# Attention kernel on one core: the end of the last group, with a's last products behind b's and the second half's b part added on GpSimd

## The chip, the cores and the metric

The kernel runs on one core of a Trainium2 chip. The time is that of one execution on the device, in microseconds (us); before the change it is 2299.06 us, the median of 3 runs (2298.87 to 2299.11). The engines are TensorE (PE; its weight loads are PEld), VectorE (DVE), ScalarE (ACT), GpSimd (POOL) and SyncE (SP, which issues most DMAs). An engine's name with a q (SPq, PEldq) is its sequencer, which handles waits, loads of registers and branches.

## The reference

```
q = x Wq + bq;  k = x Wk + bk;  v = x Wv + bv          # x is 4 x 64 x 64 x 256, N = 4096
pq, pk, pv = q, k, v, each reshaped to (B, -1, N)
attention = softmax(pq^T pk) over the keys m
out = pv attention^T, reshaped to x's shape
return gamma * out + x                                   # gamma is one number
```

For each of the 4 images, x and the result count as a matrix of 256 rows and 4096 columns. Everything is float32.

## The kernel before, in words

**Splitting.** TensorE multiplies in a rounded float32 format (F32R). Each operand is therefore split in a high part h, a low part l and a part d that holds a combination of both, and a float32 product is made of three products. For the attention they are gathered in two sums: `a` (products of h and of l) and `b` (products of d). The result is gam2 * a + gam1 * b, where gam1 and gam2 carry gamma and the factors of the split (lines 651 and 652).

**Units.** The queries of an image are cut in 8 groups of 512 columns, the keys in 16 blocks of 256. A *unit* n is one group with one block; there are 4 x 8 x 16 = 512 units, 0 to 511, and the loop at line 701 goes over them. For a unit, `cross` and `energy` make the energies on TensorE and exponentiate them on ScalarE (x); `upper` makes h on ScalarE; `halves` adds x to the group's sum s on VectorE (line 415), and makes l and d there (lines 430 and 432). After a group's last unit, `whole` adds the two halves of s (line 421). `attend(n, j, order)` multiplies with v: j = 0 and 1 are the two halves of the result's rows, and `order` says which of h, l, d (0, 1, 2) are multiplied, in which order. With h and l it adds to `now["a", j]`, with d to `now["b", j]`; both lie in PSUM and gather over the 16 units of a group. Each part is two matmuls of 128x512.

**Order.** The program is written in the order in which each engine executes it (manual schedule): every engine works through its own list, and waits on semaphores where a tile comes from another engine. In a turn of the loop, TensorE does attend(n, 0) and later attend(n, 1); `halves(n + 1)` stands between them.

**The end.** For all groups but the last, the sums are taken out of PSUM by `emptied` and finished by `finish` in pieces, by DMAs and VectorE, beside the next group's work. The last group has no next one; at unit 511 the loop calls `finish_last(n, xr)` (line 521) and stops. There:
- four matmuls of s with ones (zp, lines 525 to 529) give the sums of the exponentials with the queries on the partitions; line 532 takes the reciprocals into rall;
- attend(511, 0) is multiplied; ScalarE scales a of the first half into y0 (line 535);
- `inside` (lines 518 and 519) and line 538 test whether all reciprocals of all groups are in range, into zs;
- four matmuls with the identity (rp, line 541) spread the reciprocals over all partitions, in PSUM; one (np, line 549) adds up zs;
- attend(511, 1) is multiplied, its b part first; ScalarE scales b of the second half into y1 (line 551);
- VectorE adds b to y0 (552), sets the flag `again` from np (553), multiplies y0 by rp (554), adds it to x's first half in xr (555), and SyncE stores that half (556);
- the same for the second half (557 to 560).

x's last group was loaded into xr at unit 506 (line 712). Behind all this every engine reads `again` and branches (line 764): if a reciprocal was out of range, a second, plain version of the whole computation runs; with these inputs it is jumped over. 

**Tiles that matter here.** zp and rp share two PSUM buffers with the energies (tag "e"); np has one of its own. `o_last` is one buffer in SBUF, with y0 and y1. The tiles of tag "x" are two buffers in SBUF of 128 x 2 x 512, used by turns; the last exponentials lay in them.

Of the kernel before, what the change touches and what calls it, by code (L numbers as in the profile page):

```python
# [9 lines left out]
F32 = mybir.dt.float32  # L10
F32R = mybir.dt.float32r
I32 = mybir.dt.int32
AF = mybir.ActivationFunctionType
ALU = mybir.AluOpType
AX = mybir.AxisListType
# [5 lines left out]
def kernel(  # L21
# [36 lines left out]
    nc = tc.nc  # L58
    B, W, H, C = x.shape
    P = 128  # L60
# [21 lines left out]
    NB = 512  # L82
    NJ = NB // P
    NG = N // NB
    NU = NM // 2
    STEPS = NG * NU
# [5 lines left out]
    ones = ones_r.bitcast(F32)  # L92
    again = const.tile([P, 1], I32, name="again")
    gam3 = const.tile([P, 3], F32, name="gam")
    gam, gam1, gam2 = (gam3[:, i : i + 1] for i in range(3))
    zs = const.tile([P, 1], F32, name="zs")
    rall = const.tile([P, B * NG, NJ], F32, name="rall")
# [3 lines left out]
    with ExitStack() as fast:  # L101
# [5 lines left out]
        ppool = pool("ppool", 2)  # L107
        work = pool("work", 2)
        kpool = pool("kpool", 3)
        dram = pool("dram", 2, space=DRAM)  # L110
        ps_e = pool("ps_e", 2, space=PSUM)
# [35 lines left out]
        qd, kf, vf, units, loads, now = {}, {}, {}, {}, {}, {}  # L147
# [259 lines left out]
        def halves(n):  # L407
            if n >= B * STEPS:
                return
            x, h = units[n]  # L410

            def summed():
                if n % NU:
                    s = now["s"]
                    nc.vector.tensor_tensor(s, s, x, ALU.add)  # L415
                else:
                    now["s"] = x

            def whole():
                s = now["sum"] = now["s"]  # L420
                nc.vector.tensor_tensor(s[:, 0, :], s[:, 0, :], s[:, 1, :], ALU.add)

            after = 0 < n < 5
            if not after:
                summed()
            if n % NU == NU - 1:
                whole()
            ld = ppool.tile([P, 2, 2, NB], F32R, tag="ld", name=f"ld_{n}")
            l, d = ld[:, 0], ld[:, 1]
            nc.vector.tensor_tensor(l, x, h.bitcast(F32), ALU.subtract)  # L430

            nc.vector.scalar_tensor_tensor(  # L432
                d, h.bitcast(F32), 1.0 + E, x, ALU.mult, ALU.subtract
            )
            if n == 2:
                next(vs)
                next(vs, None)
            if after:
                summed()
            units[n] = h, l, d  # L440

        def attend(n, j, order=(0, 1, 2)):

            t = n % NU
            if t == 0:
                for i, c in enumerate("ab"):
                    pool, tag = ps_o, f"{c}{j}"
                    if j and n >= (B - 1) * STEPS and n // NU % 2 == 0:
                        pool, tag = now["banks"][i]
                    now[c, j] = pool.tile([P, NB], F32, tag=tag, name=f"{c}{j}_{n // NU}")  # L450
            for f in order:
                to = now["ab"[f == 2], j]
                for i in (1, 0) if f == 1 else (0, 1):
                    nc.tensor.matmul(  # L454
                        to,
                        vall[:, t, i, f, j * P : (j + 1) * P],
                        units[n][f][:, i, :],
                        start=(t == 0 and i == 0 and f != 1),
                        stop=(t == NU - 1 and f != 0 and i == f // 2),
                        skip_group_check=True,  # L460
                    )
# [54 lines left out]
        def inside(ok, r):  # L516

            nc.vector.tensor_scalar(ok, r, 1.0 / Z_HIGH, None, ALU.is_ge)
            nc.vector.scalar_tensor_tensor(ok, r, 1.0 / Z_LOW, ok, ALU.is_le, ALU.mult)

        def finish_last(n, xr):

            b, g = B - 1, NG - 1
            S = now["sum"][:, 0, :]
            zp = ps_e.tile([P, NJ, 2], F32, tag="e", name="zp")
            for j in range(NJ):
                nc.tensor.matmul(  # L527
                    zp[:, j, :], S[:, j * P : (j + 1) * P], ones[:, :2], start=True, stop=True
                )
            attend(n, 0)  # L530
            r4 = rall[:, B * NG - 1, :]
            nc.vector.reciprocal(r4, zp[:, :, 0])
            o = work.tile([P, 2, NB], F32, tag="o", name="o_last", bufs=1)
            y0, y1 = o[:, 0, :], o[:, 1, :]
            nc.scalar.activation(y0, now["a", 0], AF.Identity, scale=gam2)  # L535
            ok = ppool.tile([P, 2, NB], F32, tag="x", name="last")[:, 0, : B * NG * NJ]
            inside(ok, rall.rearrange("p n j -> p (n j)"))
            nc.vector.tensor_reduce(zs, ok, AX.X, ALU.min)
            rp = ps_e.tile([P, NB], F32, tag="e", name="rp")
            for j in range(NJ):  # L540
                nc.tensor.matmul(
                    rp[:, j * P : (j + 1) * P],
                    r4[:, j : j + 1].to_broadcast([P, P]),
                    ident,
                    start=True,
                    stop=True,
                )
            np_ = ps_p.tile([P, 1], F32, tag="p0", name="np")
            nc.tensor.matmul(np_, ones, zs, start=True, stop=True)
            attend(n, 1, (2, 0, 1))  # L550
            nc.scalar.activation(y1, now["b", 1], AF.Identity, scale=gam1)
            nc.vector.scalar_tensor_tensor(y0, now["b", 0], gam1, y0, ALU.mult, ALU.add)  # L552
            nc.vector.tensor_scalar(again, np_, P - 0.5, None, ALU.is_lt)
            nc.vector.tensor_tensor(y0, y0, rp, ALU.mult)
            nc.vector.tensor_tensor(xr[:, 0, :], xr[:, 0, :], y0, ALU.add)
            nc.sync.dma_start(og[b, g][:, 0], xr[:, 0, :])
            nc.vector.scalar_tensor_tensor(y1, now["a", 1], gam2, y1, ALU.mult, ALU.add)  # L557
            nc.vector.tensor_tensor(y1, y1, rp, ALU.mult)  # L558
            nc.vector.tensor_tensor(xr[:, 1, :], xr[:, 1, :], y1, ALU.add)
            nc.sync.dma_start(og[b, g][:, 1], xr[:, 1, :])  # L560


        R = 2 * STEPS // NI
# [137 lines left out]
        for n in range(B * STEPS):  # L701
            b, u = divmod(n, STEPS)
            g, t = divmod(u, NU)
            final = n == B * STEPS - 1
            if n == 0:
                image(1)
                load_x(1, 0)
            if u == STEPS - 5 and b + 2 < B:
                image(b + 2)
            if n == B * STEPS - 6:  # L710
                xr = ppool.tile([P, 2, NB], F32, tag="s", name="xr")
                nc.sync.dma_start(xr, xg[b, g])
            cross(n + LOOK)
            turn = t == NU - 1 and not final
            if t == 0 and n:
                upper(n + LOOK - 1)
            p = n - 3 + 2 * (n > 17)
            step(p, "act")
            late = n >= (B - 1) * STEPS
            if not final:  # L720
                attend(n, 0)
            if late and 1 <= t <= 2 and n > 1:
                emptied(n - 1 - t, 1, done, t - 1)
            energy(n + LOOK)
            load_k(n + LOOK + 3)
            store()
            if t == 0 and n:
                done = full
            if turn:
                emptied(n, 0)  # L730
            else:
                upper(n + LOOK)
            step(p, "pe")
            if turn:
                active.append(finish(n // NU, now["o"], now["s"]))
            if t == 0 and n and not late:
                emptied(n - 1, 1, done, vector=True)
            halves(n + 1)
            step(p, "dve")
            if final:  # L740
                finish_last(n, xr)
                break
            attend(n, 1)
            full = now["a", 1], now["b", 1]
            if n == 17:
                for engine in ("act", "pe", "dve"):
                    step(p + 1, engine)
                    step(p + 2, engine)
            if t == 8 and n + NU < B * STEPS:
                load_q(*divmod(n // NU + 1, NG))  # L750
            for m in range(2 * NU):
                c, r = divmod(n + NU - 3 - 13 * m // 16, STEPS)
                if r == 0 and 0 < c < B:
                    load_v(c, m // 2, m % 2)
            proceed()
            for to, pieces in xloads[:6]:
                nc.sync.dma_start(to, pieces)
            del xloads[:6]

    NB = 512  # L760
    NG = N // NB
    NJ = NB // P
# [213 lines left out]
```

## Time and profile before

| | |
|---|---|
| median of 3 runs | 2299.06 us |
| profiled execution: time | 2299.0 us |
| profiled execution: span, first to last instruction | 2297.2 us |
| mean granted clock of TensorE | 0.999 |
| TensorE's share of the chain that ended last | 99% |
| last matmul pair of 128x512 starts | 2287.69 us |
| last store issued by SyncE | 2290.66 us |

The profile is one execution, taken by the hardware. Its lines give busy time in us for each engine and its share of the span; x10568 is a number of instructions. In the timeline a row is: start in us from the span's beginning, duration in us, engine, line of the kernel, operation, tile written <- tiles read, shapes, and how many instructions the row merges. A [0.46 <-DVE v L160] at its end says that the engine sat idle for 0.46 us before it, until that work of VectorE released it. The chain of work that ended last is followed back from the last instruction, at each step to what released it, or to the instruction before it on its engine. The rows of a single line (L764, the flag) give min/median/max of the duration in ns, and the first and the last start in us.

### The profile page before, as it was taken

What the parts mean: (1) busy time and instruction counts of PE and PEld (TensorE: products, weight loads), DVE (VectorE), ACT (ScalarE), POOL (GpSimd) and SP (SyncE); (2) the same over time, 40 slices, a digit from 0 to 9 for tenths busy, and PEclk for the clock granted to TensorE, in tenths of its full rate; (3) what the DMA queues carried; (4) which work ended last, traced back from release to release, by engine and by line L of the source; (5) the groups of instructions that cost most, each with busy time, mean ns of one, the idle gap of its engine ahead of it and who ended that gap; (6) DMA issues with size and microseconds to landing.
All of it is one profiled execution on the core that took longest, in us unless ns stands there. A gap on an engine that the chain in (4) does not pass through costs nothing.

```text
span 2297.2 us, 31906 instructions
## 1 busy us (share of the span) xinstructions
PE 2286.7 (100%) x10568; PEld 1912.6 (83%) x10568; DVE 2160.5 (94%) x2222; ACT 1794.1 (78%) x2917; POOL 445.5 (19%) x747
## 2 busy tenths in 40 slices
PE   9999999999999999999999999999999999999998
PEld 9888888888888888888888888888888888888886
DVE  8999999999999999999999999999999899888888
ACT  7778777787777777777777778777788777888885
POOL 7111111111331111111122111111112211111110
PEclk9999999999999999999999999999999999999999
DMA  8567766677996777666799667766689855555554
GB/s 274 162 172 208 199 177 167 172 209 197 278 280 191 198 193 196 177 171 180 211 294 287 177 179 205 199 177 171 170 226 301 241 149 144 135 139 144 151 142 107
DMA packets 305743, 445.31 MB, mean 194 GB/s; under 512 B 129698, under 2 KB 183204, under 8 KB 305572
## 3 DMA queue, kind: packets, MB, share of 16 engines
q0 software_dynamic: 105584, 296.79, 48.3%
q1 hardware_dynamic: 199568, 146.14, 20.6%
q8 instruction: 87, 1.43, 0.2%
q14 instruction: 84, 0.69, 0.1%
q10 hardware_dynamic: 420, 0.26, 0.0%
HBM read 313.79 MB, written 112.26 MB: 185 GB/s over the span
## 4 chain that ended last, share of the span: by engine, by line
PE 99%; DVE 0%; ACT 0%; issue 0%; POOL 0%; DVEq 0%; POOLq 0%
PE a L454 40%; PE e L395 20%; PE b L454 20%; PE e L380 10%; PE qv L269 5%; PE v L286 3%; PE xt L231 0%; PE wp L141 0%; ACT qv L304 0%; PE zp L527 0%; DVE o_last L557 0%; DVE o_last L552 0%; DVE qv L297 0%; DVE o_last L558 0%; ACT o_last L535 0%
## 5 line engine op out<-in xcount | busy, mean ns | idle before, releaser
L398 ACT ACTIVATE x<-e 128x512 f32<-128x512 f32 x960 | 522.0, 596 | 323.6 <-PE e L395 323.6
L381 ACT ACTIVATE e<-e 128x512 f32<-128x512 f32 x1024 | 546.3, 570 | 114.8 <-PE e L380 114.8
L454 PE MATMUL a<-h,v 128*128 128x512 f32 x2048 | 631.3, 389 | 0.0
L454 PE MATMUL b<-ld,v 128*128 128x512 f32 x2048 | 630.9, 389 | 0.0
L454 PE MATMUL a<-ld,v 128*128 128x512 f32 x2048 | 630.8, 389 | 0.0
L415 DVE TENSOR_TENSOR s<-s,x 128x1024 f32<-128x1024 f32 x480 | 583.9, 1217 | 47.8 <-ACT x L398 46.2
L367 POOL DMA_DIRECT2D k<-kf x512 | 273.0, 533 | 1799.3 <-PE e L395 1753.0
L430 DVE TENSOR_TENSOR ld<-x,h 128x1024 fp32r<-128x1024 f32 x480 | 584.3, 1217 | 22.1 <-ACT h L404 22.1
L432 DVE SCALAR_TENSOR_TENSOR ld<-h,x 128x1024 fp32r<-128x1024 f32 x480 | 584.3, 1217 | 0.0
L395 PE MATMUL e<-q,k 128*128 128x512 f32 x2048 | 547.6, 389 | 0.0
L404 ACT ACTIVATE h<-x 128x1024 fp32r<-128x1024 f32 x480 | 510.7, 1064 | 14.2
L454 PEld LDWEIGHTS a<-ld,v 128*128 128x128 f32 x2048 | 384.4, 188 | 80.4
L454 PEld LDWEIGHTS b<-ld,v 128*128 128x128 f32 x2048 | 384.2, 188 | 80.5 <-DVE ld L432 0.5
L395 PEld LDWEIGHTS e<-q,k 128*128 128x128 f32 x2048 | 384.2, 188 | 79.7
L454 PEld LDWEIGHTS a<-h,v 128*128 128x128 f32 x2048 | 381.3, 188 | 76.0
L380 PE MATMUL e<-q,k 128*128 128x512 f32 x1024 | 315.4, 389 | 0.0
L380 PEld LDWEIGHTS e<-q,k 128*128 128x128 f32 x1024 | 192.0, 188 | 39.9
L322 DVE SCALAR_TENSOR_TENSOR f<-f,qv 128x512 fp32r<-128x512 f32 x128 | 85.7, 680 | 0.3
L269 PE MATMUL qv<-wf,xf 128*128 128x256 f32 x576 | 77.2, 285 | 0.3
L269 PEld LDWEIGHTS qv<-wf,xf 128*128 128x128 f32 x576 | 73.7, 191 | 3.4 <-issue 0.5
L430 DVE TENSOR_TENSOR ld<-s,h 128x1024 fp32r<-128x1024 f32 x32 | 39.3, 1227 | 36.8 <-ACT h L404 34.1
L167 DVE SCALAR_TENSOR_TENSOR vf<-vf,v 128x512 fp32r<-128x512 f32 x96 | 65.3, 680 | 0.0
(89 smaller groups left out, 1100.1 us busy)
## 6 DMA issues: line engine op xcount, KB each, us to landing
k<-kf POOLq DMA_DIRECT2D x512, 384.0 KB, 3.6
vf<-vf SPq DMA_DIRECT2D x96, 384.0 KB, 4.8
v<-vf POOLq DMA_DIRECT2D x96, 384.0 KB, 6.1
kf<-f SPq DMA_DIRECT2D x128, 192.0 KB, 3.9
qd<-f SPq DMA_DIRECT2D x124, 192.0 KB, 3.9
q<-qd POOLq DMA_DIRECT2D x31, 768.0 KB, 5.5
o<-o POOLq DMA_DIRECT2D x31, 512.0 KB, 5.3
o<-in_x_dram POOLq DMA_DIRECT2D x31, 512.0 KB, 6.5
```

The costliest lines, as they stand in the source:

```text
L269: nc.tensor.matmul(to[:, s, :], left, right.rearrange("p s a -> p (s a)") if w else right, start=(f == 2 and s == k == 0), stop=(f == 1 an ...
L322: nc.vector.scalar_tensor_tensor(f[:, :, :, j, :], h.bitcast(F32), s, y, ALU.mult, op)
L367: nc.gpsimd.dma_start(t, kf[b, u % NU])
L380: nc.tensor.matmul(e, *forms(n, i, 2), start=True, stop=False, skip_group_check=True)
L381: nc.scalar.mul(e, e, -REST)
L395: nc.tensor.matmul(e, *forms(n, i, f), start=False, stop=(f == 1), skip_group_check=True)
L398: nc.scalar.activation(x[:, i, :], e, AF.Exp, scale=(1.0 + E) ** 3 / E)
L404: nc.scalar.activation(h, units[n], AF.Identity, scale=UPPER)
L415: nc.vector.tensor_tensor(s, s, x, ALU.add)
L430: nc.vector.tensor_tensor(l, x, h.bitcast(F32), ALU.subtract)
L432: nc.vector.scalar_tensor_tensor(d, h.bitcast(F32), 1.0 + E, x, ALU.mult, ALU.subtract)
L454: nc.tensor.matmul(to, vall[:, t, i, f, j * P : (j + 1) * P], units[n][f][:, i, :], start=(t == 0 and i == 0 and f != 1), stop=(t == NU - ...
```

## The change

Seven edits, all at the end of the last group:
- the second half of unit 510 is split: its b products run where attend(510, 1) stood, inside `halves(511)`, and its a products go to the end; the loop no longer calls attend(510, 1);
- zp and its reciprocal move into `halves(511)`, between the l and the d of unit 511;
- TensorE's order in `finish_last` becomes: a of the first half, rp, b of the first half, b of the second half, then a's products of the second half for unit 510 and 511, with np among them;
- ScalarE copies rp to SBUF (rs) in place of scaling b of the second half;
- VectorE multiplies b of the second half by gam1 and rs in one instruction (line 563 of the changed kernel), and GpSimd adds that to x's second half (line 564); the rest of the second half is a times gam2 times rs (568) and one addition (569);
- y0 is multiplied by rs, in SBUF, where it was multiplied by rp, in PSUM (565);
- the flag `again` is set last (571).

```diff
--- before.py
+++ after.py
@@ -428,7 +428,9 @@
             ld = ppool.tile([P, 2, 2, NB], F32R, tag="ld", name=f"ld_{n}")
             l, d = ld[:, 0], ld[:, 1]
             nc.vector.tensor_tensor(l, x, h.bitcast(F32), ALU.subtract)
-
+            if n == B * STEPS - 1:
+                attend(n - 1, 1, (2,))
+                sums()
             nc.vector.scalar_tensor_tensor(
                 d, h.bitcast(F32), 1.0 + E, x, ALU.mult, ALU.subtract
             )
@@ -438,6 +440,15 @@
             if after:
                 summed()
             units[n] = h, l, d
+
+        def sums():
+            S = now["sum"][:, 0, :]
+            zp = ps_e.tile([P, NJ, 2], F32, tag="e", name="zp")
+            for j in range(NJ):
+                nc.tensor.matmul(
+                    zp[:, j, :], S[:, j * P : (j + 1) * P], ones[:, :2], start=True, stop=True
+                )
+            nc.vector.reciprocal(rall[:, B * NG - 1, :], zp[:, :, 0])
 
         def attend(n, j, order=(0, 1, 2)):
 
@@ -521,21 +532,8 @@
         def finish_last(n, xr):
 
             b, g = B - 1, NG - 1
-            S = now["sum"][:, 0, :]
-            zp = ps_e.tile([P, NJ, 2], F32, tag="e", name="zp")
-            for j in range(NJ):
-                nc.tensor.matmul(
-                    zp[:, j, :], S[:, j * P : (j + 1) * P], ones[:, :2], start=True, stop=True
-                )
-            attend(n, 0)
+            attend(n, 0, (0, 1))
             r4 = rall[:, B * NG - 1, :]
-            nc.vector.reciprocal(r4, zp[:, :, 0])
-            o = work.tile([P, 2, NB], F32, tag="o", name="o_last", bufs=1)
-            y0, y1 = o[:, 0, :], o[:, 1, :]
-            nc.scalar.activation(y0, now["a", 0], AF.Identity, scale=gam2)
-            ok = ppool.tile([P, 2, NB], F32, tag="x", name="last")[:, 0, : B * NG * NJ]
-            inside(ok, rall.rearrange("p n j -> p (n j)"))
-            nc.vector.tensor_reduce(zs, ok, AX.X, ALU.min)
             rp = ps_e.tile([P, NB], F32, tag="e", name="rp")
             for j in range(NJ):
                 nc.tensor.matmul(
@@ -545,19 +543,32 @@
                     start=True,
                     stop=True,
                 )
+            attend(n, 0, (2,))
+            attend(n, 1, (2,))
+            o = work.tile([P, 2, NB], F32, tag="o", name="o_last", bufs=1)
+            y0, y1 = o[:, 0, :], o[:, 1, :]
+            nc.scalar.activation(y0, now["a", 0], AF.Identity, scale=gam2)
+            rs = ppool.tile([P, 2, NB], F32, tag="x", name="rs")[:, 0, :]
+            nc.scalar.copy(rs, rp)
+            last = ppool.tile([P, 2, NB], F32, tag="x", name="last")
+            ok, y2 = last[:, 0, : B * NG * NJ], last[:, 1, :]
+            inside(ok, rall.rearrange("p n j -> p (n j)"))
+            nc.vector.tensor_reduce(zs, ok, AX.X, ALU.min)
             np_ = ps_p.tile([P, 1], F32, tag="p0", name="np")
+            attend(n - 1, 1, (0,))
             nc.tensor.matmul(np_, ones, zs, start=True, stop=True)
-            attend(n, 1, (2, 0, 1))
-            nc.scalar.activation(y1, now["b", 1], AF.Identity, scale=gam1)
+            attend(n - 1, 1, (1,))
+            attend(n, 1, (0, 1))
             nc.vector.scalar_tensor_tensor(y0, now["b", 0], gam1, y0, ALU.mult, ALU.add)
-            nc.vector.tensor_scalar(again, np_, P - 0.5, None, ALU.is_lt)
-            nc.vector.tensor_tensor(y0, y0, rp, ALU.mult)
+            nc.vector.scalar_tensor_tensor(y1, now["b", 1], gam1, rs, ALU.mult, ALU.mult)
+            nc.gpsimd.tensor_tensor(xr[:, 1, :], xr[:, 1, :], y1, ALU.add)
+            nc.vector.tensor_tensor(y0, y0, rs, ALU.mult)
             nc.vector.tensor_tensor(xr[:, 0, :], xr[:, 0, :], y0, ALU.add)
             nc.sync.dma_start(og[b, g][:, 0], xr[:, 0, :])
-            nc.vector.scalar_tensor_tensor(y1, now["a", 1], gam2, y1, ALU.mult, ALU.add)
-            nc.vector.tensor_tensor(y1, y1, rp, ALU.mult)
-            nc.vector.tensor_tensor(xr[:, 1, :], xr[:, 1, :], y1, ALU.add)
+            nc.vector.scalar_tensor_tensor(y2, now["a", 1], gam2, rs, ALU.mult, ALU.mult)
+            nc.vector.tensor_tensor(xr[:, 1, :], xr[:, 1, :], y2, ALU.add)
             nc.sync.dma_start(og[b, g][:, 1], xr[:, 1, :])
+            nc.vector.tensor_scalar(again, np_, P - 0.5, None, ALU.is_lt)
 
 
         R = 2 * STEPS // NI
@@ -740,7 +751,8 @@
             if final:
                 finish_last(n, xr)
                 break
-            attend(n, 1)
+            if n < B * STEPS - 2:
+                attend(n, 1)
             full = now["a", 1], now["b", 1]
             if n == 17:
                 for engine in ("act", "pe", "dve"):
```

In the changed kernel lines from 431 on have other numbers than before: `halves`' d is L434, the products of `attend` are L465, zp is L448, its reciprocal L451, rp L539, np L559, y0 L550, the copy rs L552, and the flag is read in L776.

## The prediction

> **What bounds the kernel now.** I read the page first, then the chain of work that ended last, then the timeline of the last 16 us.
>
> ```profile
> span 2297.2 us, 31906 instructions
> PE 2286.7 (100%) x10568; PEld 1912.6 (83%) x10568; DVE 2160.5 (94%) x2222; ACT 1794.1 (78%) x2917; POOL 445.5 (19%) x747
> PE 99%; DVE 0%; ACT 0%; issue 0%; POOL 0%; DVEq 0%; POOLq 0%
> ```
>
> The page says that TensorE is busy nearly all the time and makes 99% of the chain. The change takes no product away: it gives the last ones another order. So only what happens behind TensorE, in the last microseconds, can change. There the chain of waits looks like this (start, duration, work):
>
> ```profile
> 2284.30 1.06 PE a L454 x4
> 2285.39 0.69 ACT o_last L535
> 2286.11 0.75 DVE o_last L552
> 2286.93 0.69 DVE o_last L554
> 2287.64 0.69 DVE xr L555
> 2288.44 0.76 DVE o_last L557
> 2289.22 0.70 DVE o_last L558
> 2289.95 0.69 DVE xr L559
> ```
>
> The end is not set by the last products. It leaves TensorE after the sums a of the first half, goes to ScalarE, and then through VectorE without a hole. Six VectorE instructions of 0.69 to 0.76 us, and a small one, stand in a row. The last products are these (start, duration, engine, line):
>
> ```profile
> 2281.99 0.62 PE L454 MATMUL a<-h,v 128*128 128x512 f32 x2
> 2282.01 1.22 DVE L430 TENSOR_TENSOR ld<-x,h 128x1024 fp32r<-128x1024 f32 x1
> 2283.14 1.22 DVE L432 SCALAR_TENSOR_TENSOR ld<-h,x 128x1024 fp32r<-128x1024 f32 x1
> 2283.35 0.95 PE L527 MATMUL zp<-ones,s 128*128 128x2 f32 x8
> 2284.16 0.72 PE L454 MATMUL a<-h,v 128*128 128x512 f32 x2
> 2284.34 0.18 DVE L532 RECIPROCAL rall<-zp 128x4 f32<-128x4 f32 x1
> 2284.72 0.63 PE L454 MATMUL a<-ld,v 128*128 128x512 f32 x2
> 2285.19 0.62 PE L454 MATMUL b<-ld,v 128*128 128x512 f32 x2
> 2285.65 1.05 PE L541 MATMUL rp<-ident,rall 128*128 128x128 f32 x8
> 2286.54 0.28 PE L549 MATMUL np<-zs,ones 128*128 128x1 f32 x2
> 2286.68 0.71 PE L454 MATMUL b<-ld,v 128*128 128x512 f32 x2
> 2287.23 0.63 PE L454 MATMUL a<-h,v 128*128 128x512 f32 x2
> 2287.69 0.62 PE L454 MATMUL a<-ld,v 128*128 128x512 f32 x2
> ```
>
> They end at 2287.69 + 0.62 = 2288.31, and VectorE gets to L557 at 2288.44, behind L555, which ended at 2288.33. TensorE and VectorE are level there, so work taken off VectorE *behind* that point pays only while VectorE is not late *at* that point. Behind the last VectorE instruction comes this:
>
> ```profile
> 2290.66 0.34 SPq L560 DMA_DIRECT2D out_dram<-xr  x1
> L764 PEldq COMPARE_BRANCH  x1: 3490/3490/3490, 2287.6 to 2287.6; - x1
> L764 ACTq COMPARE_BRANCH  x1: 50/50/50, 2288.0 to 2288.0; - x1
> L764 ACTq EVENT_SEMAPHORE  x1: 17/17/17, 2290.8 to 2290.8; - x1
> L764 SPq TENSOR_LOAD <-again x1: 548/548/548, 2291.1 to 2291.1; - x1
> L764 SPq COMPARE_BRANCH  x1: 50/50/50, 2291.7 to 2291.7; - x1
> L764 SPq EVENT_SEMAPHORE  x8: 17/17/17, 2294.4 to 2294.9; - x8
> ```
>
> SyncE issues the last store, reads the flag "again", branches, and goes on 2.7 us after the branch (2291.7 to 2294.4); ScalarE, which has no store to wait for, also needs 2.8 us (2288.0 to 2290.8). So the tail, 2297.2 - 2290.66 = 6.5 us, hangs on SyncE's own list. It moves with the last store, microsecond for microsecond. The forecast is therefore one question: when does VectorE finish the last addition?
>
> **The change, part by part.** *TensorE.* The same products in another order, with the distances of the rows above: 0.46 from pair to pair, 0.81 from zp to the next pair, 0.56 for the first pair behind zp, 0.89 for rp, 0.55 for the first pair behind rp or np. The b products of unit 510's second half stand at 2281.99; zp at 2282.45 (it needs L421's sum, 2281.40 + 0.69 = 2282.09, below), done at 2283.40; a of the first half at 2283.26 and 2283.82, done at 2284.45; rp at 2284.29, done at 2285.34; b of the first half at 2285.18, done at 2285.89; b of the second at 2285.73, done at 2286.36; then a's held-back products at 2286.19 and 2286.79 with np between, and the last two pairs at 2287.34 and 2287.80. TensorE ends at 2288.42 instead of 2288.31: plus 0.1, covered by VectorE below.
>
> ```profile
> 2281.40 0.69 DVE L421 TENSOR_TENSOR s<-s 128x512 f32<-128x512 f32 x1
> 30.22 0.68 DVE L160 SCALAR_TENSOR_TENSOR v<-v,qv 128x512 fp32r<-128x512 f32 x1
> 30.98 1.30 POOL L163 TENSOR_TENSOR v<-v 128x512 fp32r<-128x512 f32 x1 [0.46 <-DVE v L160]
> 8.23 0.69 DVE L178 SCALAR_TENSOR_TENSOR wf<-wf,scaled 128x512 fp32r<-128x512 f32 x1
> 8.28 0.74 POOL L639 TENSOR_SCALAR bvs<-bvs 128x2 f32<-128x2 f32 x1
> 9.39 0.22 POOL L652 TENSOR_SCALAR gam<-gam 128x1 f32<-128x1 f32 x1
> 9.44 0.69 DVE L180 TENSOR_TENSOR wf<-scaled,wf 128x512 fp32r<-128x512 f32 x1
> 2285.14 0.29 DVE L538 TENSOR_REDUCE zs<-last 128x1 f32<-128x128 f32 x1
> 2286.86 0.16 DVE L553 TENSOR_SCALAR again<-np 128x1 int32<-128x1 f32 x1
> ```
>
> *Reciprocal ahead of d.* VectorE now waits for zp between l and d of unit 511: reciprocal at 2283.44. d starts some 0.1 behind that, overlapping it as L432 overlaps L430 (1.13 apart, 1.22 each), and ends near 2284.8, 0.4 later than now. Queued behind it are b's products (2285.18) and the range test, which needs 0.9 (from the reciprocal's end, 2284.52, to L538's, 2285.43, now) and is out near 2285.7, ahead of np at 2286.65. Cost nothing; the cover is 0.4 us.
>
> *ScalarE.* y0 now runs at 2284.49 to 2285.18. The copy of rp into rs takes rp at 2285.38 and, by L535's 0.69, ends at 2286.07. The old L551 is gone. VectorE needs rs at about 2286.6, so this costs nothing, with a cover of 0.5.
>
> *VectorE's row.* It starts when b of the first half is done, 2285.89 + 0.04 = 2285.93 (before: 2286.11). L562 takes 0.75, as L552 does. L563 (b of the second half times gam1 times rs) takes 0.75 and does not need L562, so by the 0.09 overlap it ends at T = 2287.35. L565 and L566 (0.69 each) finish the first half; L568 takes 0.75 and the last addition 0.69. Before, L552, L553, L554, L555, L557, L558, L559 stood here. So the count of large instructions is six on both sides: L558's product is gone from the end, but L563 is new ahead of it. What is removed behind the last product comes back in front of it. If nothing else interferes, L566 ends at 2288.70, after TensorE's 2288.42: VectorE is now the bound and the fusion gains only the earlier start and the overlaps. Last addition done: 2285.93 + 4.32 (six durations) - 0.1 (overlaps less gaps of 0.03) = 2290.12, store at 2290.14, against 2290.66: a gain of 0.5.
>
> *GpSimd.* New: x plus y1 for the second half, 128x512. L163 prices it at 1.30, starting 0.08 after VectorE's release (30.90 to 30.98). Uncontended it would run from T + 0.08 to 2288.73 and be waited for by nobody, since the last addition comes at 2289.4. But at that time VectorE runs L565, then L566, each with two operands in SBUF (rs was copied out of PSUM). The rows above show what this does: L639, an operation on 2 columns, started 0.05 after L178, whose two operands lie in SBUF, and ended 0.10 after it (9.02 against 8.92). It took 0.74; L652, with 1 column, took 0.22. So GpSimd was held until VectorE was through. L163's rows run beside VectorE instructions with one operand in PSUM, and show no such thing. Here then GpSimd gets in only when L565 has ended, T + 0.63 = 2287.98, and has 1.30 - 0.22 + 0.10 = 1.18 left: done at 2289.16.
>
> Who goes next when L565 ends, GpSimd, which has waited for 0.5 us, or L566, which can start 0.03 later? No row of before shows VectorE held by GpSimd: L180 started 0.05 into L652 and took its usual 0.69, but those 0.2 us are too few to tell. The bounds are a hold of 0 and of 1.18. I take the full hold, since L639 was held whole and not slowed, and the one that asked first should go first. Then L566 runs 2289.16 to 2289.85, L568 to 2290.52, the last addition 2290.55 to 2291.24, the store at 2291.26: 0.60 later than now. The Trainium skill ("SBUF — State Buffer", section "Who interferes with whom") speaks against this change in the same place: a VectorE instruction with two SBUF inputs contends with a GpSimd instruction that reads SBUF, the one that issues first has the shared ports for its whole instruction, and the other blocks fully. The trace agrees for GpSimd behind VectorE (0.74 against 0.22); for VectorE behind GpSimd it shows nothing yet.
>
> *The flag.* L571 now comes behind the last addition, so all five engines read "again" only then. SyncE's read comes anyway 0.34 + 0.1 behind the store's issue, and L571 (0.16, as L553) fits in. The others were done long before; now TensorE reads at about 2291.4 and needs 0.5 + 3.5, until 2295.4, while SyncE, moved by 0.60, clears its semaphores until 2295.5. Cost nothing, barely. One GpSimd instruction is added; no DMA.
>
> Sum against the profiled execution, which took 2299.0 at a span of 2297.2 (so 1.8 lies around the span) and is within 0.1 of the median 2299.06: 2299.06 + 0.60 = 2299.7.
>
> **The rivals.** *VectorE keeps the port.* GpSimd is held by L565 and again by L566, until 2288.70, and ends at 2289.88. L568 (2288.62 to 2289.37, one operand in PSUM) passes; the last addition waits for GpSimd: 2289.92 to 2290.61. Store at 2290.63, no change: 2299.0. For it speaks that VectorE's instructions follow in 0.03; against it that GpSimd is already waiting.
>
> *No contention at these sizes*, or one below 0.3 us. Gain 0.5: 2298.5. For it: L180 beside L652. Against it: L639's 0.74. This would mean that the change does what it says.
>
> *Slower beyond the bound: the late flag.* All five engines branch together. If their 2.7 us behind the branch were served one after another, SyncE as fifth would lose 4 x 2.7 = 10.8 us: 2310. It decides as soon as SyncE's 2.7 grows, since nothing covers it; with the 0.60 it passes the bound of 4.6 when the 2.7 becomes 6.7. Against it: now ScalarE (2288.0 to 2290.8) and TensorE (3.49 from 2287.6) go through it at the same time and neither doubles.
>
> **How the numbers follow.** Full hold of VectorE, 2299.7: 0.45, by itself 2299.3 to 2300.1. VectorE keeps the port, 2299.0: 0.25. No contention, 2298.5: 0.27. Late flag: 0.02. The last 0.01 is for a gain that I don't see. The range reaches from the no-contention case less 0.3 to the full hold plus 0.5: 2298.2 to 2300.2. A measurement of this kernel can tell about 0.2% (4.6 us) from no change; all three main cases lie well inside, hence same 0.97, slower 0.02, faster 0.01.
>
> **What would show it.** Right: in the timeline of the changed kernel the first-half addition (L566) starts close behind L565 but lasts near 1.9 us, or starts only at 2289.2, the GpSimd addition lasts 1.7 instead of 1.3, and the last store stands near 2291.3. The second rival shows L566 at 0.69, a GpSimd addition of 2.4, and the last addition waiting for it. The third shows 1.3 for GpSimd and a store near 2290.1. TensorE's last pair should start within 0.1 of 2287.8, and the tail behind the store stay at 6.5 us. I am wrong altogether if the tail grows by microseconds, if y1 waits for rs, or if zp or b's products of the first half show a wait.

## The result and the profile after

The changed kernel takes 2303.14 us (median of 22 runs, 2302.96 to 2304.68), the kernel before 2299.07 (22 runs). The ratio is 1.0017, with a 95% interval of 1.0011 to 1.0023: 4.07 us slower, 0.18%, just inside the bound of 0.2% and far outside the forecast range. A few executions of every kernel here, the one before too, lie 1.3 to 2.5 us above the others (and one of the kernel before at 4291.5); they widen the intervals, so medians are compared below. The profiled execution took 2303.0 us. Its page:

```profile
span 2301.2 us, 31910 instructions
PE 99%; DVE 0%; issue 0%; POOL 0%; ACT 0%; DVEq 0%; POOLq 0%
```

The span grew by 4.0, so the loss lies inside it. Up to 2280 us the two traces agree within 0.15. The last compute instructions of the changed kernel, from its timeline:

```profile
2284.97 1.18 PE L465 MATMUL b<-ld,v 128*128 128x512 f32 x4
2285.79 0.75 DVE L562 SCALAR_TENSOR_TENSOR o_last<-b,gam,o_last 128x512 f32<-128x512 f32 x1 [0.29 <-PE b L465]
2286.46 0.74 DVE L563 SCALAR_TENSOR_TENSOR o_last<-b,gam,rs 128x512 f32<-128x512 f32 x1
2287.12 0.68 DVE L565 TENSOR_TENSOR o_last<-o_last,rs 128x512 f32<-128x512 f32 x1
2287.29 1.64 POOL L564 TENSOR_TENSOR xr<-xr,o_last 128x512 f32<-128x512 f32 x1 [18.27 <-DVE o_last L563]
2287.61 0.62 PE L465 MATMUL a<-ld,v 128*128 128x512 f32 x2
2287.83 1.65 DVE L566 TENSOR_TENSOR xr<-xr,o_last 128x512 f32<-128x512 f32 x1
2289.41 0.74 DVE L568 SCALAR_TENSOR_TENSOR last<-a,gam,rs 128x512 f32<-128x512 f32 x1
2290.24 0.69 DVE L569 TENSOR_TENSOR xr<-xr,last 128x512 f32<-128x512 f32 x1
2290.85 0.15 DVE L571 TENSOR_SCALAR again<-np 128x1 int32<-128x1 f32 x1
2290.97 0.34 SPq L570 DMA_DIRECT2D out_dram<-xr  x1
```

TensorE ends as before. GpSimd's addition and VectorE's L566 are both too long, as forecast: GpSimd ends 1.13 behind L565 (2288.93 against 2287.80), and L566 ends 0.55 behind GpSimd. But the last store is issued at 2290.97, only 0.31 later than before. Yet the span is 4.0 longer: the tail behind the store grew from 6.5 us to 10.2. The rows of the flag's line show who does what in it. First the rows before, from the line of the flag and the line of the program's end (L972), where the engines signal each other through semaphores, the closing barrier:

```profile
L764 POOLq TENSOR_LOAD <-again x1: 491/491/491, 2287.0 to 2287.0; - x1
L764 POOLq INC_SWDGE_SEM  x1: 1802/1802/1802, 2287.9 to 2287.9; - x1
```

```profile
L972 POOLq EVENT_SEMAPHORE  x4: 17/17/17, 2296.4 to 2297.1; - x4
L972 POOLq DRAIN  x3: 46/107/6602, 2289.8 to 2296.9; - x3
L972 SPq DRAIN  x3: 7/7/13, 2295.8 to 2296.6; - x3
```

Then the same lines of the changed kernel:

```profile
L776 POOLq TENSOR_LOAD <-again x1: 491/491/491, 2291.0 to 2291.0; - x1
L776 POOLq INC_SWDGE_SEM  x1: 1802/1802/1802, 2291.9 to 2291.9; - x1
L776 SPq COMPARE_BRANCH  x1: 50/50/50, 2292.0 to 2292.0; - x1
L776 SPq EVENT_SEMAPHORE  x8: 17/17/17, 2295.2 to 2295.7; - x8
```

```profile
L984 POOLq EVENT_SEMAPHORE  x4: 17/17/17, 2300.4 to 2301.1; - x4
L984 POOLq DRAIN  x3: 46/107/6602, 2293.8 to 2300.9; - x3
L984 SPq DRAIN  x3: 7/7/13, 2296.5 to 2300.6; - x3
```

GpSimd reads the flag (TENSOR_LOAD), branches, spends 1.80 us in INC_SWDGE_SEM and then 6.60 us in its first DRAIN: before from 2289.8 to 2296.4, now from 2293.8 to 2300.4, each time its first semaphore of the closing barrier follows there. What these two instructions wait for, no run here shows. SyncE reached its own DRAIN at 2295.8 before and at 2296.5 now, and waits. The waits of SyncE's queue, before and after, count that (us in total, times, longest; the name behind the arrow is the last to signal in the barrier, not the late one):

```profile
SPq L972 <- PEq L972: 1.3, 2, 0.7
```

```profile
SPq L984 <- PEq L984: 4.5, 2, 4.0
```

So already before, SyncE waited 0.7 us at the end. The engine that came last was GpSimd. It ends a fixed time behind its read of the flag, 10.2 us to the end of the span both times (2287.0 to 2297.2, 2291.0 to 2301.2). That read moved by 4.0, because the flag is set at 2290.85 instead of 2286.86.

### The profile page after: what moved, and what is told of

It reads as the page before. It is cut to its first block, busy times and chain, and to the rows that moved or that the text cites. A ratio compares the mean times of both kernels' runs of the same rounds, so it can differ in the third digit from the quotient of the medians.

```text
span 2301.2 us, 31910 instructions
## 1 busy us (share of the span) xinstructions
PE 2286.0 (99%) x10568; PEld 1911.8 (83%) x10568; DVE 2160.7 (94%) x2222; ACT 1794.5 (78%) x2917; POOL 447.1 (19%) x748
## 4 chain that ended last, share of the span: by engine, by line
PE 99%; DVE 0%; issue 0%; POOL 0%; ACT 0%; DVEq 0%; POOLq 0%
PE a L465 40%; PE e L395 20%; PE b L465 20%; PE e L380 10%; PE qv L269 5%; PE v L286 3%; PE xt L231 0%; ACT qv L304 0%; DVE xr L566 0%; POOL scaled L174 0%; POOL bvs L130 0%; PE rp L539 0%; PE zp L448 0%; DVE wf L178 0%; DVE xr L569 0%
## 5 line engine op out<-in xcount | busy, mean ns | idle before, releaser
L465 PE MATMUL a<-h,v 128*128 128x512 f32 x2048 | 631.3, 389 | 0.0
L465 PE MATMUL a<-ld,v 128*128 128x512 f32 x2048 | 631.0, 389 | 0.0
L465 PE MATMUL b<-ld,v 128*128 128x512 f32 x2048 | 630.5, 389 | 0.0
L415 DVE TENSOR_TENSOR s<-s,x 128x1024 f32<-128x1024 f32 x480 | 583.1, 1215 | 48.1 <-ACT x L398 46.4
L434 DVE SCALAR_TENSOR_TENSOR ld<-h,x 128x1024 fp32r<-128x1024 f32 x480 | 583.3, 1215 | 0.0
L465 PEld LDWEIGHTS a<-ld,v 128*128 128x128 f32 x2048 | 384.3, 188 | 80.4
L465 PEld LDWEIGHTS b<-ld,v 128*128 128x128 f32 x2048 | 384.2, 188 | 80.5 <-DVE ld L434 0.5
L465 PEld LDWEIGHTS a<-h,v 128*128 128x128 f32 x2048 | 381.3, 188 | 76.0
```

The costliest lines, as they stand in the source:

```text
L434: nc.vector.scalar_tensor_tensor(d, h.bitcast(F32), 1.0 + E, x, ALU.mult, ALU.subtract)
L465: nc.tensor.matmul(to, vall[:, t, i, f, j * P : (j + 1) * P], units[n][f][:, i, :], start=(t == 0 and i == 0 and f != 1), stop=(t == NU - ...
```

## The experiments

Three theories. *GpSimd*: the end is GpSimd's read of the flag plus 10.2. *Branch*: five engines that branch at once slow each other. *Port*: the time goes in GpSimd and VectorE blocking each other. The first four kernels tell them apart.

**e1: the changed kernel with the flag set early.**

```diff
             nc.gpsimd.tensor_tensor(xr[:, 1, :], xr[:, 1, :], y1, ALU.add)
+            nc.vector.tensor_scalar(again, np_, P - 0.5, None, ALU.is_lt)
...
-            nc.vector.tensor_scalar(again, np_, P - 0.5, None, ALU.is_lt)
```

> The changed kernel with the flag set right behind the GpSimd addition's issue instead of last. GpSimd theory (the program ends a fixed 10.2 us after GpSimd reads the flag: 2287.0 to 2297.2 before, 2291.0 to 2301.2 after): GpSimd reads it once its addition is over, at about 2288.9 (or at 2287.4, if its sequencer reads ahead of the addition), so the span is 2299.1 (2297.6), the time 2301.0 (2299.5). Branch theory (five engines that branch at once slow each other by 4 us): ScalarE and TensorE branch early again, SyncE's 3.2 us behind its branch fall back to 2.7, and the span is the store's time plus 6.5, 2297.5; time 2299.3. Port theory (GpSimd and VectorE blocking each other costs it all): no change, 2303.1.

Measured: 2299.45 us, ratio 1.0003 (0.9994 to 1.0013): 3.7 of the 4.07 us are back. The port theory falls, since the clash is still there (GpSimd's addition at 1.71 and VectorE's L567 at 1.64 below). From the timeline and the flag's line of e1:

```profile
2287.42 1.71 POOL L564 TENSOR_TENSOR xr<-xr,o_last 128x512 f32<-128x512 f32 x1 [18.27 <-DVE again L565]
2288.03 1.64 DVE L567 TENSOR_TENSOR xr<-xr,o_last 128x512 f32<-128x512 f32 x1
2291.16 0.34 SPq L571 DMA_DIRECT2D out_dram<-xr  x1
```

```profile
L776 POOLq TENSOR_LOAD <-again x1: 496/496/496, 2287.4 to 2287.4; - x1
```

GpSimd's sequencer reads the flag while its addition still runs, the lower of the two forecasts, and the span ends 10.2 behind that read (2297.6). The branch theory forecast nearly the same time, 2299.3, so this run alone doesn't settle it.

**e2: the kernel before, with only the flag moved behind the last addition.** 
```diff
             nc.vector.scalar_tensor_tensor(y0, now["b", 0], gam1, y0, ALU.mult, ALU.add)
-            nc.vector.tensor_scalar(again, np_, P - 0.5, None, ALU.is_lt)
...
             nc.sync.dma_start(og[b, g][:, 1], xr[:, 1, :])
+            nc.vector.tensor_scalar(again, np_, P - 0.5, None, ALU.is_lt)
```

> The kernel before with nothing changed but the flag, set behind the last addition. GpSimd theory: all read it at about 2290.9, the span becomes 2301.1 and the time 2302.9, nearly all of the change's loss. Branch theory: the same here, since all five branch together. Port theory: no loss, 2299.1, since GpSimd computes nothing.

Measured: 2302.78 us, ratio 1.0017 (1.0007 to 1.0026). One moved instruction of 0.16 us costs 3.8 us, and no GpSimd operation is needed for it: the port theory falls again. The branch theory forecast a loss too. GpSimd in its trace:

```profile
L764 POOLq TENSOR_LOAD <-again x1: 493/493/493, 2290.9 to 2290.9; - x1
```

The span ended at 2301.1, again 10.2 later.

**e7: only GpSimd late. e8: only ScalarE and TensorE late.** Both are the kernel before with small operations added behind the last store; all else, the flag too, stays where it was. One diff shows both; the comments name the run that has the line.

```diff
             nc.sync.dma_start(og[b, g][:, 1], xr[:, 1, :])
+            nc.gpsimd.tensor_scalar(bvs[:, :1], xr[:, 1, :1], 1.0, None, ALU.mult)        # e7
+            nc.scalar.activation(bias[:, :1], xr[:, 1, :1], AF.Identity, scale=1.0)       # e8
+            nc.tensor.matmul(np_, ones, xr[:, 1, :1], start=True, stop=True)              # e8
```

> The kernel before with one added GpSimd operation on one column that waits for the last addition, so that GpSimd alone reads the flag late (about 2291.0); the other engines read it when they did. GpSimd theory: span 2301.2, time 2303.0. Branch theory: the others are not disturbed; time 2299.1 to 2299.6.

> The kernel before with one added small operation each on ScalarE and TensorE that waits for the last addition, so that these two read the flag late (about 2291), and GpSimd as early as it did. GpSimd theory: time 2299.1, within 0.3. Branch theory: four engines branch together; time up by 2 us or more, 2301 to 2303.

Measured: e7 2302.81 us, ratio 1.0017 (1.0008 to 1.0027); e8 2299.07, ratio 1.0001 (0.9991 to 1.0010). The flag's line in e7:

```profile
L765 PEldq TENSOR_LOAD <-again x1: 487/487/487, 2287.0 to 2287.0; - x1
L765 ACTq TENSOR_LOAD <-again x1: 462/462/462, 2287.4 to 2287.4; - x1
L765 POOLq TENSOR_LOAD <-again x1: 494/494/494, 2290.6 to 2290.6; - x1
```

and in e8:

```profile
L766 POOLq TENSOR_LOAD <-again x1: 490/490/490, 2287.3 to 2287.3; - x1
L766 ACTq TENSOR_LOAD <-again x1: 467/467/467, 2290.9 to 2290.9; - x1
L766 PEldq TENSOR_LOAD <-again x1: 489/489/489, 2290.9 to 2290.9; - x1
L766 PEldq COMPARE_BRANCH  x1: 3987/3987/3987, 2291.5 to 2291.5; - x1
```

GpSimd late and the rest early costs all of it; ScalarE and TensorE late and GpSimd early costs nothing. The branch theory falls as the cause. (SyncE does go on later where all five branch together: 3.1 to 3.2 us behind its branch in the changed kernel, e2 and e12, 2.7 before; but it then waits for GpSimd. TensorE's branch takes 3.99 us in e8 and 3.49 before, but that company makes it longer isn't shown: with the same three engines branching together it takes 4.03 in e1 and 3.47 in e4.)

**e4: e1 without two operands in SBUF beside GpSimd's addition. e12: the same edit in the changed kernel, flag last.**

```diff
-            nc.vector.tensor_tensor(y0, y0, rs, ALU.mult)
-            nc.vector.tensor_tensor(xr[:, 0, :], xr[:, 0, :], y0, ALU.add)
+            nc.vector.tensor_tensor(rp, y0, rp, ALU.mult)
+            nc.vector.tensor_tensor(xr[:, 0, :], xr[:, 0, :], rp, ALU.add)
```

> The kernel of e1 (flag early), but the first half's product is formed from rp and written to rp, in PSUM, so that neither VectorE instruction beside GpSimd's addition has two operands in SBUF. Port theory (the 1.7 us of GpSimd's addition and the 1.6 us of the first half's addition come from two operands in SBUF): GpSimd's addition 1.30, the first half's addition 0.69, last store 0.9 us earlier than e1's 2291.2, at about 2290.2. A rival (GpSimd's addition is slow for another reason, or disturbs VectorE whatever it reads): both stay at 1.6 to 1.7. GpSimd theory for the time: its read of the flag stays at 2287.4, so the span stays at 2297.6 and the time at 2299.4, although the store is 1 us earlier; if the store set the end, 2298.4.

> The changed kernel, flag last as it is there, with the first half's product formed from rp and written to rp in PSUM (e4's edit alone). GpSimd theory: without the 1.0 us by which its addition holds VectorE, the chain up to the flag ends 1.0 earlier (the last addition near 2290.0 instead of 2290.9), GpSimd reads at 2290.1 instead of 2291.0, and the time falls by 0.9 to 1.0, to 2302.2: the clash is a quarter of the loss, the flag's place three quarters. If the clash were hidden behind something else: 2303.1.

Measured: e4 2299.47 us, ratio 1.0002 (0.9993 to 1.0011); e12 2302.23, ratio 1.0014 (1.0005 to 1.0023). The timeline of e4:

```profile
2287.42 0.69 DVE L566 TENSOR_TENSOR rp<-o_last,rp 128x512 f32<-128x512 f32 x1
2287.52 1.28 POOL L564 TENSOR_TENSOR xr<-xr,o_last 128x512 f32<-128x512 f32 x1 [18.27 <-DVE again L565]
2288.14 0.69 DVE L567 TENSOR_TENSOR xr<-xr,rp 128x512 f32<-128x512 f32 x1
2290.31 0.34 SPq L571 DMA_DIRECT2D out_dram<-xr  x1
```

its GpSimd's read of the flag:

```profile
L776 POOLq TENSOR_LOAD <-again x1: 498/498/498, 2287.5 to 2287.5; - x1
```

and the timeline of e12, with GpSimd's read of the flag:

```profile
2289.89 0.15 DVE L571 TENSOR_SCALAR again<-np 128x1 int32<-128x1 f32 x1
2290.00 0.34 SPq L570 DMA_DIRECT2D out_dram<-xr  x1
```

```profile
L776 POOLq TENSOR_LOAD <-again x1: 491/491/491, 2290.1 to 2290.1; - x1
```

With one operand in PSUM both engines run at their usual 0.69 and 1.28, side by side, in e12 too: the operands' place makes the clash. In e4 the last store comes 0.85 earlier than in e1, and the time doesn't move, since GpSimd reads the flag no earlier. In e12 the flag itself hangs on the store's chain, and the hold of VectorE (1.65 - 0.69 = 0.96) shows up nearly in full, 0.91 us. So of the loss of 4.07, some 0.9 goes with the clash, which delays the flag, and 3.2 is left for the flag's place. The split depends on the order: with the flag moved first 3.7 come back (e1), and then the clash costs nothing (e4).

**e5: the kernel before, with the flag as early as the new order allows.** zp, its reciprocal and the range test come as early as in the changed kernel, np between the two b products, the flag ahead of the first instruction of VectorE's tail; nothing on GpSimd (`sums` and the split of unit 510 in `halves` as in the changed kernel, not repeated in the diff). **e10: e4 repaired**, with b of the second half first, so that GpSimd's addition and the flag come earlier; its diff, the second one, is against e4.

```diff
-            S = now["sum"][:, 0, :]
-            zp = ps_e.tile([P, NJ, 2], F32, tag="e", name="zp")
...
-            attend(n, 0)
+            attend(n, 0, (0, 1))
...
+            attend(n, 0, (2,))
...
             nc.tensor.matmul(np_, ones, zs, start=True, stop=True)
-            attend(n, 1, (2, 0, 1))
+            nc.vector.tensor_scalar(again, np_, P - 0.5, None, ALU.is_lt)
+            attend(n, 1, (2,))
+            attend(n - 1, 1, (0, 1))
+            attend(n, 1, (0, 1))
             nc.scalar.activation(y1, now["b", 1], AF.Identity, scale=gam1)
             nc.vector.scalar_tensor_tensor(y0, now["b", 0], gam1, y0, ALU.mult, ALU.add)
-            nc.vector.tensor_scalar(again, np_, P - 0.5, None, ALU.is_lt)
             nc.vector.tensor_tensor(y0, y0, rp, ALU.mult)
```

```diff
-            attend(n, 0, (2,))
             attend(n, 1, (2,))
+            attend(n, 0, (2,))
...
-            attend(n - 1, 1, (0,))
             nc.tensor.matmul(np_, ones, zs, start=True, stop=True)
+            attend(n - 1, 1, (0,))
...
-            nc.vector.scalar_tensor_tensor(y0, now["b", 0], gam1, y0, ALU.mult, ALU.add)
             nc.vector.scalar_tensor_tensor(y1, now["b", 1], gam1, rs, ALU.mult, ALU.mult)
-            nc.gpsimd.tensor_tensor(xr[:, 1, :], xr[:, 1, :], y1, ALU.add)
             nc.vector.tensor_scalar(again, np_, P - 0.5, None, ALU.is_lt)
+            nc.vector.scalar_tensor_tensor(y0, now["b", 0], gam1, y0, ALU.mult, ALU.add)
+            nc.gpsimd.tensor_tensor(xr[:, 1, :], xr[:, 1, :], y1, ALU.add)
```

> The kernel before with the sums zp, their reciprocal and the range test taken earlier, as in the changed kernel, and the flag set ahead of VectorE's first instruction of the tail; nothing on GpSimd, the rest as before. GpSimd theory: it reads the flag at about 2286.0, its part would end the program at 2296.2, and then SyncE's branch behind the last store (2290.6, nearly as before) is the bound, some 0.6 earlier than now: span 2296.6, time 2298.4. If the store set the end of the kernel before, no change: 2299.0.

> The kernel of e4 with b of the second half ahead of b of the first on TensorE and VectorE, np behind them, and the flag right behind the second half's b part, so that GpSimd's addition and its read of the flag are released at about 2286.7. GpSimd theory: span 2286.85 + 10.2 = 2297.05, time 2298.8, 0.2 under the kernel before, with the last store at 2290.2. If the store decided: 2298.4.

Measured: e5 2298.48 us, ratio 0.9996 (0.9987 to 1.0005); e10 2298.93, ratio 0.9999 (0.9990 to 1.0008). Neither interval excludes 1, but 9 of e5's 11 runs lie below the lowest of the 33 runs of the kernel before (2298.85): 0.58 us by the medians, as forecast. e10's store stands 0.4 earlier than the kernel before's, yet e10 gains 0.1 by the medians: its GpSimd reads the flag at 2286.7, 0.3 earlier, and the span ends 10.2 behind that (the profiled execution, at 2298.66, is e10's fastest).

```profile
2290.26 0.34 SPq L571 DMA_DIRECT2D out_dram<-xr  x1
```

```profile
L776 POOLq TENSOR_LOAD <-again x1: 498/498/498, 2286.7 to 2286.7; - x1
```

e5's profiled execution took 2300.97, 2.5 above its median; most of that lies ahead of the tail (unit 511's d starts at 2285.91, in e11, below, at 2283.74), so only distances are read in it. The flag's and the end's lines of e5:

```profile
L773 POOLq TENSOR_LOAD <-again x1: 497/497/497, 2288.6 to 2288.6; - x1
```

```profile
L981 POOLq EVENT_SEMAPHORE  x4: 17/17/17, 2298.3 to 2299.0; - x4
L981 POOLq DRAIN  x3: 46/107/6602, 2291.3 to 2298.8; - x3
L981 SPq DRAIN  x3: 7/7/13, 2298.2 to 2298.5; - x3
```

Here GpSimd is through at 2291.3 + 6.6 = 2297.9, SyncE at 2298.2: for the first time SyncE comes last, and the span ends 10.5 behind GpSimd's read. This is the second bound.

**e11: e5 without the last addition.** It leaves out x in the second half of the last group, and stores y1 as it is.

```diff
-            nc.vector.tensor_tensor(xr[:, 1, :], xr[:, 1, :], y1, ALU.add)
-            nc.sync.dma_start(og[b, g][:, 1], xr[:, 1, :])
+            nc.sync.dma_start(og[b, g][:, 1], y1)
```

> The kernel of e5 without the last addition of x to the second half: y1 is stored as it is, so that the last store comes 0.7 us earlier (2289.9) and nothing else changes. If SyncE's branch behind the store is the bound of e5, the time falls until GpSimd's read decides: by 0.4, to 2298.0. If GpSimd's read still bounds e5, no change against e5.

Measured: 2298.30 us, ratio 0.9995 (0.9986 to 1.0005), 0.18 less than e5, where 0.4 was forecast. In its trace GpSimd is last again:

```profile
L980 POOLq DRAIN  x3: 46/107/6602, 2289.1 to 2296.3; - x3
L980 SPq DRAIN  x3: 7/7/13, 2295.4 to 2296.0; - x3
```

2289.1 + 6.6 = 2295.7 against 2295.4. That the store sets e5's end fits the sign, but the two sets of runs overlap (the lowest is 2298.11 in both), so how far the second bound lies behind the first is not shown to better than 0.2; by e5's one trace it is 0.3 (2298.2 against 2297.9).

## Why the prediction was wrong

**The step that failed** is "So the tail, [...] hangs on SyncE's own list. It moves with the last store, microsecond for microsecond", and with it the last step, on the flag: "The others were done long before [...] Cost nothing, barely." SyncE's list was long, but not the longest. The prediction counted TensorE's, ScalarE's and SyncE's instructions behind the flag, and left out GpSimd's, whose DRAIN of 6.6 us stood in the profile of before and whose end, 2296.4, was later than anything of SyncE's except its wait for it. GpSimd's read had a margin below zero: it was the bound already, so all 4.0 us of delay counted (e2, e7), and the end moved with the flag, not with the store (e4). The prediction had named the sign for this: it is wrong altogether "if the tail grows by microseconds", and the tail grew from 6.5 to 10.2.

**TensorE's part** held: the same products in nearly the same time, last pair at 2287.61 (forecast 2287.80). That is 0.19 early where the prediction allowed 0.1, but 0.13 of it was there ahead of the change (L415 starts at 2280.01, before at 2280.14). **VectorE's row** began at 2285.79 (forecast 2285.93). The reciprocal ahead of d, the copy rs and the range test cost nothing, as worked out.

**GpSimd against VectorE** held in its mechanism, a little over-sized: GpSimd done at 2288.93 (2289.16), L566 at 2289.48 (2289.85), store at 2290.97 (2291.26). About 0.15 of each gap is the earlier start. The one that had waited went first, and VectorE was held for 0.96 us, nearly the whole rest of GpSimd's instruction (forecast 1.18). The Trainium skill's rule ("SBUF — State Buffer", section "Who interferes with whom": the first to issue has the shared ports for its instruction, the other blocks) agrees, in both directions now: 1.64 against 1.28 for GpSimd, 1.65 against 0.69 for VectorE, and neither with an operand in PSUM (e4). But the store's delay of 0.31 was itself hidden behind GpSimd's way out; the clash cost 0.9 only by delaying the flag (e12).

**The rival of the late flag** had the right place and the wrong mechanism, with a chance of 0.02. It priced branches served one after another, at 2310. Measured, SyncE goes on 3.2 behind its branch instead of 2.7 (2292.0 to 2295.2), and then waits 4.0 anyway; e8 shows that the branches did not set the end. The Trainium skill ("Runtime: NRT & Kernel Launch", section "Instruction fetch mechanics") says that a taken branch out of the fetched window waits for a fetch of its target. The 2.7 to 3.2 us would fit that, and in the changed kernel's trace an instruction queue moves 5 packets between 2292.8 and 2296; but GpSimd goes on 0.2 behind the same branch (2287.6 to 2287.8 before), so whether SyncE's wait is such a fetch is not shown.

The time stayed within 0.2% of the kernel before, but the range ended at 2300.2, 2.9 us below what was measured: the sum had no term for what GpSimd does behind its read of the flag.

## What to carry to other kernels

Behind the last store, look at every engine's sequencer, the idle one above all, and ask who signals last in the closing barrier; the page's busy times and chain don't show it. A flag that all engines read before they branch is on the path of the engine with the longest way out, so set it as early as its inputs allow; here an instruction of 0.16 us moved to the end cost 3.8 us. Where GpSimd is to work beside VectorE, look where VectorE's operands lie: in this kernel GpSimd's addition was free only where VectorE's instructions had one operand in PSUM (e4, e12).

## What the runs showed of the hardware

- GpSimd's way out of this program is constant: read, branch, INC_SWDGE_SEM of 1.80 us and a DRAIN of 6.60 us, the same within 0.01 in all eleven traces; 10.1 to 10.2 us from the read to the end of the span in the ten where it is last. Why they take so long stays open.
- GpSimd's sequencer read the flag while its engine's last operation still ran: in e1 at 2287.4, at the start of an addition that ended at 2289.13, and the addition cost its way out nothing.
- Two VectorE operands in SBUF beside a GpSimd addition held both engines in turn: 1.28 became 1.64 to 1.71, 0.69 became 1.64 to 1.65.
